# Mixtures, gathers and a router step of a mixture-of-experts kernel set to other places in the program

## The chip, the cores and the metric

The kernel runs on one core of a Trainium2 chip. The metric is the device time of one execution in microseconds; below, "time" is the median of the runs shown, and "span" is the time from the first to the last instruction in one profiled execution. The engines are TensorE (PE; its weight loads are PEld), VectorE (DVE), ScalarE (ACT), GpSimd (POOL) and SyncE (SP), which only issues DMAs here.

## The reference

Input x is 8 batches of 1024 tokens with 512 features, all in 32 bit. The block is `x = x + attention(layernorm(x))`, then `x = x + experts(layernorm(x))`.

- Attention has 16 heads of 32. Queries, keys and values are sines and cosines (a table of 2048 steps with linear interpolation) of angles that are linear in the feature and in the token's place; then causal softmax and the sum over values, and a last sine plus cosine.
- Experts: a router (512 x 8) and softmax choose 2 of 8 experts for each token. Each expert takes the first 160 tokens of each batch that chose it (its capacity), so 1280 rows in all, computes `relu(rows @ W1 + b1) @ W2 + b2` with a hidden size of 2048, and the result times the gate is added to the token's row.

## The kernel before

**Attention.** 32 rounds, one for each batch and each chunk of 128 features. The router of a batch runs as a generator (`router`, L779) whose steps are spread over the rounds of the next batch. For the last batch it runs inside the experts' first part, as `ending` (L1503).

**Experts.** The rows of an expert are done in two parts: 768 rows (even parts, 0, 2, ...) and 512 rows (odd parts), so 16 parts. Each product of matrices is done with seven block products instead of eight, so rows, weights and results are mixed by sums and differences:

- `gather` (L1072) fetches a part's rows in tiles of 128 by indirect DMA on POOL (`fetch`, L1078), six tiles for an even part and four for an odd one. It transposes each on TensorE (L1117), copies it to `xe` on DVE (L1118) and mixes the rows on DVE (L1124 to L1127). The pool of fetched tiles, `gp`, has two buffers.
- `mix_w1` (L1144) makes four differences of a tile of W1 on DVE (L1153; in the first six groups of the first part on POOL).
- `layer1` (L1158) does one of eight groups of hidden features: seven products of 2 matmuls (L1169, 384 or 256 columns) and what follows them on DVE and ACT (L1184 to L1202).
- `mix_w2` (L1043) mixes the eight tiles of W2 on DVE, four operations a tile (L1050 to L1053).
- `layer2` (L1205) does a block of 128 x 2 rows: seven products of 8 matmuls (L1214, 256 columns), sums, bias and gate on DVE (L1230, L1231, L1246 to L1258), and an indirect DMA with addition for each half (`send`, L1236). An even part has three blocks, an odd one two. The first three products of a block use W2 as loaded; the fourth uses the third output of `mix_w2`.

The profile counts a 32-bit matmul as two records.

**What sets the order.** On PE, DVE, ACT and SP the program's own order holds (`manual_schedule`). POOL's instructions are put in order by a scheduler, but for some that are marked to stay in program order: the gathers of parts 1 and 2, the sends of part 0, and the W1 mixtures on POOL. Work beside the products is generators: after each product, `product` calls `next` on them, so a `yield` is a distance of one product. In layer two the generator is the gather of the next part; in the first part's layer one it is `ending`, which ends by loading the slot table (`fetch_slots`, L989). Behind the first part's layer one, `find_rows` (L1069) turns the slot table into row numbers for the odd parts' gathers, on DVE.

PSUM: `ps_p` has six buffers, one for a product; `ps_tr` two, for transposes and the last router. In the last router, `rows` (L807) normalises a tile of tokens on DVE and stores it through SP (L813), `features` transposes two tiles on TensorE (L823) and copies them on ACT (L824), and `sums` multiplies by the router's weights (L869). The buffers for normalised tiles (`xn2`) are two.

The loop over parts, as it stands (L1309 to L1323):

```python
elif i == 0 and q == NHQ - 2:
    mixes = mix_w2(0)
    for _ in range(2):
        next(mixes)
...
if i == 0:
    find_rows(1)
rest(mixes)
aside = start(gather(i + 1), box) if i + 1 < len(chunks) else iter(())
if i == 0:
    aside = behind(2, aside)
for block in range(nh):
    layer2(i, block, hs, aside)
rest(aside)
if i + 1 < len(chunks):
    mix_w1(i + 1, 0)
```

Of the kernel before, what the change touches and what calls it, by code (L numbers as in the profile page):

```python
# [73 lines left out]
def preln_attn_moe_kernel(  # L74
# [133 lines left out]
    def two_banks():  # L208
        return ps_sc.tile([P, 2, 512], F32, name="ps_s")
# [515 lines left out]
    def some(count, *gens):  # L725

        for gen in gens:
            while count and next(gen, 0) is None:
                count -= 1
# [51 lines left out]
    def router(b):  # L781
# [11 lines left out]
        last = b == B - 1  # L793
# [22 lines left out]
        def features(g):  # L816

            xT = row2.tile([P, NCH, 2 * P], F32, name="xT", bufs=1)
            if last:
                for i, xn in enumerate(ahead):  # L820
                    ps = pools["ps_tr"].tile([P, NCH, P], F32, name="ps_t")
                    for c in range(NCH):
                        nc.tensor.transpose(ps[:, c, :], xn[:, c * P : (c + 1) * P], ident)  # L823
                    copy(xT[:, :, i * P : (i + 1) * P], ps)  # L824
            else:
                ps = two_banks()
                for i, xn in enumerate(ahead):
                    for c in range(NCH):
                        at = (NCH * i + c) * 64
                        by_halves(ps[:, :, at : at + 64], xn[:, c * P : (c + 1) * P])  # L830
                for a in range(2):
                    copy(  # L832
                        xT.rearrange("p c (i a q) -> p i c a q", a=2, q=64)[:, :, :, a, :],
                        ps[:, a, :].rearrange("p (i c q) -> p i c q", i=2, q=64),
                    )
            return xT
# [47 lines left out]
        lg = None  # L884
        for g in range(NTT // 2):
            xT = features(g)
            if g + 1 < NTT // 2:
                if not last:
                    yield
                next_rows(g)  # L890
            yield
            lg = sums(g, xT, lg)
            yield
# [124 lines left out]
    chunks = []  # L1018
# [55 lines left out]
    def gather(i):  # L1074

        e, j0, nh = chunks[i]
        def fetch(xg, j):
            ins = nc.gpsimd.indirect_dma_start(  # L1078
                out=xg, out_offset=None, in_=xn2_d[i % 2],
                in_offset=bass.IndirectOffsetOnAxis(ap=source[:, e, j0 + j, None], axis=0),  # L1080
            )
            if i in (1, 2):
                tc.keep_in_program_order(ins)
            return xg

        def fetch_next(j):
            return fetch(pools["gp"].tile([P, D], F32, name="xg"), j)

        there = []
        if i == 0:  # L1090

            t = row2.tile([P, NCH, 2 * P], F32, name="xT", bufs=1).rearrange("p c t -> p (c t)")
            places = [row2.tile([P, D], F32, name="xn2") for _ in range(2)]
            places += [t[:, :D], t[:, D:]]
            there = [fetch(xg, j) for j, xg in enumerate(places)]
            yield None
            there += [fetch_next(j) for j in (4, 5)]
        xe = pools["xep"].tile([P, NCH, 2, HALF], F32, name="xe")
        for j in range(2 * nh):
            if len(there) == j:  # L1100
                there.append(fetch_next(j))
            if j or i:
                yield None
            xg = there[j]
            dst = xe[:, :, j // nh, j % nh * P : (j % nh + 1) * P]
            if i == 0:
                ps = two_banks()[:, :, : NCH * 64]
                for c in range(NCH):
                    by_halves(ps[:, :, c * 64 : (c + 1) * 64], xg[:, c * P : (c + 1) * P])
                nc.vector.tensor_copy(  # L1110
                    dst.rearrange("p c (a q) -> p c a q", a=2),
                    ps.rearrange("p a (c q) -> p c a q", q=64),
                )
            else:
                ps = pools["ps_tr"].tile([P, NCH, P], F32, name="ps_t")
                for c in range(NCH):
                    nc.tensor.transpose(ps[:, c, :], xg[:, c * P : (c + 1) * P], ident)  # L1117
                nc.vector.tensor_copy(dst, ps)  # L1118
        n = nh * P
        a11, a12 = xe[:, :2, 0, :n], xe[:, 2:, 0, :n]  # L1120
        a21, a22 = xe[:, :2, 1, :n], xe[:, 2:, 1, :n]
        s = pools["xep"].tile([P, 3, 2, HALF], F32, name="xe_s")
        s2, s3, s4 = (s[:, k, :, :n] for k in range(3))
        TT(s3, a11, a21, ALU.subtract)  # L1124
        TT(a21, a21, a22, ALU.add)
        TT(s2, a21, a11, ALU.subtract)
        TT(s4, a12, s2, ALU.subtract)  # L1127
        yield a11, a12, s4, a22, a21, s2, s3
# [13 lines left out]
    def mix_w1(i, q):  # L1142
        w = w1_tiles.pop((i, q))
        t = pools["t1p"].tile([P, 4, 2, P], F32, name="t1")  # L1144
        b11, b12 = w[:, :2, 0, :], w[:, :2, 1, :]
        b21, b22 = w[:, 2:, 0, :], w[:, 2:, 1, :]
        t1, t2, t3, t4 = (t[:, k, :, :] for k in range(4))


        apart = i == 0 and q < 6  # L1150
        mix = nc.gpsimd.tensor_tensor if apart else TT
        for to, x1, x2 in ((t1, b12, b11), (t2, b22, t1), (t3, b22, b12), (t4, b21, t2)):
            done = mix(to, x1, x2, ALU.subtract)  # L1153
            if apart:
                tc.keep_in_program_order(done)
                mixed.append(done.ins)
        t1_tiles[i, q] = b11, b21, b22, t1, t2, t3, t4
# [114 lines left out]
    def experts_begin():  # L1272
# [6 lines left out]
        mix_w1(0, 0)  # L1279

    def experts(ending):
        pools["hp"] = to_end.pool("hp", NHQ, **right)
        pools["ps_tr"] = to_end.pool("ps_tr", 2, space=PSUM, reuse_waits="tile")
        pools["ps_p"] = to_end.pool("ps_p", 6, space=PSUM, reuse_waits="tile")
        box = first_parts
        mixes = loads = iter(())
        for i, (e, j0, nh) in enumerate(chunks):
            parts, box = box[0], [None]
            hs = []
            for q in range(NHQ):  # L1290
                if i or q != NHQ - AHEAD - 1:
                    load_ahead(i * NHQ + q + AHEAD)
                some(3, loads)
                if q + 1 < NHQ:
                    mix_w1(i, q + 1)
                if q > 1:
                    for _ in range(1 if i else 3):
                        next(mixes, None)
                hs.append(layer1(i, q, parts, [ending]))
                if i == 0 and q == NHQ // 2:  # L1300
                    rest(ending)
                    to_router.close()
                    for name, bufs in (("w2p", NHQ), ("yp", 3), ("bp", 1)):
                        pools[name] = to_end.pool(name, bufs, reuse_waits="tile", **left)
                    load_ahead(NHQ - 1)
                    load_b2(0)
                    rest(load_w2(0))
                elif i == 0 and q == NHQ - 2:
                    mixes = mix_w2(0)  # L1309
                    for _ in range(2):  # L1310
                        next(mixes)
            if i == 0:
                find_rows(1)
            rest(mixes)
            aside = start(gather(i + 1), box) if i + 1 < len(chunks) else iter(())
            if i == 0:

                aside = behind(2, aside)
            for block in range(nh):
                layer2(i, block, hs, aside)  # L1320
            rest(aside)
            if i + 1 < len(chunks):
                mix_w1(i + 1, 0)  # L1323
            if i % 2 and e + 1 < E:
                load_b2(e + 1)
                loads = load_w2(e + 1)
                mixes = mix_w2(e + 1)
# [20 lines left out]
    last = None  # L1348
# [4 lines left out]
    for n in range(NCK):  # L1353
# [144 lines left out]
        last = (es[1], halves1, pos_n)  # L1498
# [5 lines left out]
    def ending():  # L1504

        o_st = o_pre(NCK - 1, pos_n)
        scatter(NTT * TOPK // 2, together=True)
        yield
        sine(o_st[1])
        square(o_st[0])  # L1510
        for _ in range(3):
            yield
        for _ in o_post(NCK - 1, o_st):
            yield
        yield
        for name in router(B - 1):
            if name == "tiles":
                scatter(together=True)

            for _ in range({"tiles": 6, "places": 5}.get(name, 1)):  # L1520
                yield
        fetch_slots(B - 2)
        scatter(together=True)
        fetch_slots(B - 1)
# [33 lines left out]
```

## Time and profile before

| | |
|---|---|
| time, median of 3 runs | 3299.44 us (3293.29 to 3300.38) |
| the profiled execution's own time | 3283.79 us |
| its span | 3282.1 us |
| mean granted TensorE clock | 0.996 |
| attention, up to about | 1272 us |
| first part, layer one | 1273 to 1362 us |
| first part, layer two | 1367 to 1445 us |
| an even and an odd part together, later on | 246.7 us |
| DMA, share of 16 engines: the queue of SP, that of POOL | 28.6%, 7.5% |
| gather, from issue to landing: least, median, most | 3.2, 3.4, 4.8 us |
| send, the same | 4.6, 4.9, 9.6 us |

How to read it: a row of the waits names the instruction that waited, the one that released it, the total, the number of times and the longest. A row of the timeline has start, length, engine, line, operation, output and inputs, count, and in brackets the idle time ahead of it and what ended it. A row of the windows has the busy time of each engine in a stretch, the TensorE clock that was granted as a share of full speed, and what the DMA engines did.

### The profile page before, as it was taken

The numbers are of one execution on the slowest core, as the hardware profiler recorded it, in microseconds if no ns is written. First come the engines' busy times: TensorE is split into PE (matmuls) and PEld (weight loads), VectorE is DVE, ScalarE is ACT, GpSimd is POOL, SyncE is SP. The second block draws the span as 40 slices with busy tenths as digits, with TensorE's granted clock in tenths as the row PEclk, the third lists the DMA queues.
The fourth block names the chain that finished last, engine by engine and source line by source line (L and its number), as shares of the span: only waits on it lengthen the run. The fifth ranks groups of instructions, "written<-read, shape, count | busy, mean of one in ns | idle before, by whom it ended". The sixth has DMA issues, their size and how long they took to land.

```text
span 3282.1 us, 48761 instructions
## 1 busy us (share of the span) xinstructions
PE 3191.8 (97%) x18942; PEld 2166.0 (66%) x18942; DVE 2252.1 (69%) x4961; ACT 1322.4 (40%) x1617; POOL 421.3 (13%) x387
## 2 busy tenths in 40 slices
PE   5999999999999999999999999999999999999998
PEld 2444444444444444688688688688688688688687
DVE  7888888778787675755855755755755755845844
ACT  7888887878787874111111111201201201201201
POOL 2000202011110213311011011011011011011010
PEclk9999999999999999999999999999999999999999
DMA  5435454553545353423323323323322322322321
GB/s 162 143 97 161 125 150 139 142 155 104 181 116 156 92 172 71 109 51 81 94 48 77 97 49 75 99 48 72 103 45 73 105 43 73 105 44 71 107 39 26
DMA packets 235254, 319.74 MB, mean 97 GB/s; under 512 B 22456, under 2 KB 155280, under 8 KB 222992
## 3 DMA queue, kind: packets, MB, share of 16 engines
q1 hardware_dynamic: 211664, 273.38, 28.6%
q0 software_dynamic: 22912, 43.22, 7.5%
q8 instruction: 150, 2.46, 0.3%
q14 instruction: 80, 0.66, 0.1%
q10 hardware_dynamic: 448, 0.02, 0.0%
HBM read 187.62 MB, written 61.82 MB: 76 GB/s over the span
## 4 chain that ended last, share of the span: by engine, by line
PE 73%; DVE 6%; issue 3%; ACT 1%; DMA 1%; SPq 0%; POOL 0%; POOLq 0%; DVEq 0%; ACTq 0%
PE ps_p L1214 28%; PE ps_p L1169 25%; PE av L713 9%; PE ps_s L679 8%; ACT e L699 1%; PE ps_t L1117 1%; PE ps_s L215 1%; DVE qk_f L520 1%; PE ps_s L693 1%; DVE t L1153 1%; DMA xg<-xn_d,source 1%; DVE qk_r L450 0%; DMA xn_d<-xn 0%; DVE xT L832 0%; DMA qk<-qk_r 0%
## 5 line engine op out<-in xcount | busy, mean ns | idle before, releaser
L699 ACT ACTIVATE e<-ps_s 128x1024 f32<-128x1024 f32 (+1 forms) x640 | 568.5, 937 | 192.7 <-PE ps_s L679 112.2
L679 PE MATMUL ps_s<-qk 64*128 64x512 f32 (+3 forms) x3072 | 596.5, 505 | 32.8 <-DMA qk<-qk_r 12.4
L1214 PE MATMUL ps_p<-w,hid 128*128 128x256 f32 x2560 | 570.3, 380 | 4.7 <-DVE hid L1187 4.7
L1214 PEld LDWEIGHTS ps_p<-w,hid 128*128 128x128 f32 x2560 | 485.0, 191 | 71.6 <-DVE hid L1187 5.3
L713 PE MATMUL av<-e,v 128*64 128x512 f32 (+3 forms) x3072 | 524.1, 490 | 0.0
L1214 PE MATMUL ps_p<-w_t,hid 128*128 128x256 f32 x1920 | 428.9, 379 | 0.0
L679 PEld LDWEIGHTS ps_s<-qk 64*128 64x128 f32 x3072 | 262.4, 188 | 219.1 <-issue 106.9
L1214 PEld LDWEIGHTS ps_p<-w_t,hid 128*128 128x128 f32 x1920 | 362.0, 190 | 47.6
L713 PEld LDWEIGHTS av<-e,v 128*64 128x64 f32 x3072 | 200.4, 137 | 283.8 <-issue 268.0
L1169 PE MATMUL ps_p<-xe_s,t 128*128 128x256 f32 (+1 forms) x1024 | 299.1, 435 | 3.6 <-DVE t L1153 3.6
L1169 PE MATMUL ps_p<-xe,w 128*128 128x256 f32 (+1 forms) x1024 | 298.8, 434 | 1.2 <-DVE hid L1187 1.0
L1169 PE MATMUL ps_p<-xe,t 128*128 128x256 f32 (+1 forms) x1024 | 296.8, 433 | 0.0
L764 POOL DMA_INDIRECT slot_d<-token,slot x128 | 158.0, 1235 | 981.4 <-issue 629.0
L1245 ACT COPY p<-ps_p 128x256 f32<-128x256 f32 x40 | 14.7, 368 | 610.1 <-PE ps_p L1214 610.1
L1169 PEld LDWEIGHTS ps_p<-xe_s,t 128*128 128x128 f32 x1024 | 194.2, 190 | 87.7 <-DVE t L1153 8.1
L1169 PEld LDWEIGHTS ps_p<-xe,w 128*128 128x128 f32 x1024 | 192.7, 190 | 84.3 <-DVE hid L1187 8.2
L1169 PEld LDWEIGHTS ps_p<-xe,t 128*128 128x128 f32 x1024 | 194.4, 190 | 80.9 <-issue 0.4
L1078 POOL DMA_INDIRECT xg<-xn_d,source x76 | 74.3, 978 | 1060.2 <-PE ps_t L1117 1045.7
L1236 POOL DMA_INDIRECT out_dram<-y,slots x80 | 126.5, 1581 | 649.3 <-DVE y L1231 620.2
L1184 ACT ACTIVATE p<-ps_p,b_t 128x256 f32<-128x256 f32 (+1 forms) x128 | 65.4, 511 | 328.3 <-PE ps_p L1169 177.2
L1188 ACT ACTIVATE hid<-hid 128x256 f32<-128x256 f32 (+1 forms) x128 | 60.1, 470 | 327.8 <-DVE hid L1187 327.8
L1201 ACT ACTIVATE hid<-hid,b_more 128x256 f32<-128x256 f32 (+1 forms) x128 | 71.8, 561 | 274.4 <-DVE hid L1200 274.4
(224 smaller groups left out, 3815.6 us busy)
## 6 DMA issues: line engine op xcount, KB each, us to landing
w<-in_L_ffn_W_dram SPq DMA_DIRECT2D x256, 256.0 KB, 3.3
w<-in_L_ffn_W_dram SPq DMA_DIRECT2D x64, 512.0 KB, 7.3
qk<-qk_c SPq DMA_DIRECT2D x124, 256.0 KB, 4.0
qk<-qk_r SPq DMA_DIRECT2D x124, 256.0 KB, 4.3
qk_base<-base_d SPq DMA_DIRECT2D x28, 1024.0 KB, 8.9
xn_d<-xn SPq DMA_DIRECT2D x72, 256.0 KB, 2.4
x_mid<-in_L_attn_x_dram SPq DMA_DIRECT2D x16, 1024.0 KB, 8.8
out_dram<-x_mid SPq DMA_DIRECT2D x8, 2048.0 KB
```

Of the source, the lines that this page charges most:

```text
L215: nc.tensor.transpose(turned[:, a, :], src[r, :], ident[r, r])
L679: nc.tensor.matmul(ps[:, a, at : at + w], lhsT=pair[r, 1, kb * P : (kb + 1) * P], rhs=pair[r, 0, q0 : q0 + w], start=at == 0, stop=not own ...
L699: nc.scalar.activation(e, ps[:, :, :n], AF.Exp, scale=UNIT * UNIT / math.sqrt(2 * DH))
L713: nc.tensor.matmul(av[a * 64 : (a + 1) * 64, q0 - 512 * h :], lhsT=vt[:, kb, 2 * pr + a, :], rhs=es[i][:, a, at : at + w], start=kb == 0, ...
L764: queued = nc.gpsimd.indirect_dma_start(out=slot_d[b], out_offset=bass.IndirectOffsetOnAxis(ap=idx, axis=0), in_=src, in_offset=None,)
L1078: ins = nc.gpsimd.indirect_dma_start(out=xg, out_offset=None, in_=xn2_d[i % 2], in_offset=bass.IndirectOffsetOnAxis(ap=source[:, e, j0 + j ...
L1169: nc.tensor.matmul(ps, lhsT=weights[:, k, :], rhs=rows[:, k, :], start=k == 0, stop=k == 1)
L1184: nc.scalar.activation(p1, product(b11, a11), AF.Identity, bias=b1_t[:, e * NHC + q : e * NHC + q + 1])
L1188: nc.scalar.activation(h11, h11, AF.Relu)
L1201: nc.scalar.activation(h12, h12, AF.Relu, bias=more)
L1214: nc.tensor.matmul(ps, lhsT=hs[k][:, part, cols], rhs=ws[k][weight], start=k == 0, stop=k == NHQ - 1,)
L1236: ins = nc.gpsimd.indirect_dma_start(out=out, out_offset=bass.IndirectOffsetOnAxis(ap=meta[:, e, jj[r], 0:1], axis=0), in_=ys[r], in_offse ...
```

## The change

Four places, all of order; no arithmetic is added or taken away.

1. `features(0)` of the last router is done one step earlier: `ending` waits five steps instead of six behind "tiles", and a `yield` is put behind the first `features`, so that the rows that follow keep their step.
2. `gather` of every part but the first: two tiles are fetched at the first step, then two steps pass before the first tile is transposed. The further tiles are fetched, in the program, right behind the transposes that free their buffer. Before, a tile was fetched one step ahead of its transposes.
3. In the first part, the three mixtures of W2 between `mix_w1(0, 7)` and the last group of layer one go; they are done with the rest, behind `find_rows(1)`. `some(2, mixes)` does the same two mixtures as the loop before it.

4. `mix_w1(i + 1, 0)` is done ahead of the last block of layer two instead of behind it.

```diff
@@ router: the loop over pairs of tiles
             xT = features(g)
+            if last and g == 0:
+                yield
             if g + 1 < NTT // 2:
@@ gather
             there += [fetch_next(j) for j in (4, 5)]
+        else:
+            there = [fetch_next(j) for j in range(2)]
+            yield None
+            yield None
         xe = pools["xep"].tile([P, NCH, 2, HALF], F32, name="xe")
         for j in range(2 * nh):
-            if len(there) == j:
-                there.append(fetch_next(j))
-            if j or i:
+            if j:
                 yield None
             xg = there[j]
@@ gather: behind the transposes and the copy of tile j
                 nc.vector.tensor_copy(dst, ps)
+            if len(there) < 2 * nh:
+                there.append(fetch_next(len(there)))
@@ experts: the loop over groups of layer one
-                if q > 1:
-                    for _ in range(1 if i else 3):
-                        next(mixes, None)
+                if i and q > 1:
+                    next(mixes, None)
@@
                     mixes = mix_w2(0)
-                    for _ in range(2):
-                        next(mixes)
+                    some(2, mixes)
@@ experts: layer two
             for block in range(nh):
+                if block == nh - 1 and i + 1 < len(chunks):
+                    mix_w1(i + 1, 0)
                 layer2(i, block, hs, aside)
             rest(aside)
-            if i + 1 < len(chunks):
-                mix_w1(i + 1, 0)
@@ ending
-            for _ in range({"tiles": 6, "places": 5}.get(name, 1)):
+            for _ in range({"tiles": 5, "places": 5}.get(name, 1)):
                 yield
```

On POOL the scheduler gives another order from the second part on. For an odd part's layer two (with the gather of the next even part) it was: four gathers (tiles three to six), a send, two gathers of the next odd part, three sends. It is: three gathers (tiles three to five), a send, a gather (tile six), a gather of the next odd part, a send, a gather of the next odd part, two sends.

## The prediction

> **What bounds the kernel now.** First the busy shares of the page, then the waits of TensorE from the last attention block on, then the timeline at the end of the first part's layer one, then busy time and granted clock in windows of 3.41 us.
>
> ```profile
> PE 3191.8 (97%) x18942; PEld 2166.0 (66%) x18942; DVE 2252.1 (69%) x4961; ACT 1322.4 (40%) x1617; POOL 421.3 (13%) x387
> ```
>
> TensorE is busy 97% of the span, and in the experts nearly without a gap: from 1548 us to the end it idles only at the W1 waits below. Of this change nothing can be gained but TensorE's waits, and they are few:
>
> ```profile
> PE ps_p L1214 <- DVE hid L1187: 4.7, 1, 4.7
> PE ps_p L1169 <- DVE t L1153: 3.6, 8, 0.6
> PE ps_t L1117 <- DMA xg<-xn_d,source: 3.3, 2, 1.8
> PE ps_t L869 <- ACT xT L824: 2.7, 1, 2.7
> PE ps_p L1169 <- DVE hid L1187: 1.0, 1, 1.0
> ```
>
> The columns are who waits for whom, us in total, times, longest. Each edit aims at one row: W2 mixtures at the first, W1 mixture at the second, gathers at the third, router step at the last two. Together they are 15.3 us, 0.46% of the time.
>
> **W1 mixture (L1153).** Four subtractions of 0.42 us go in front of the last block; they issue no DMA, and nothing else is added. TensorE waits for them eight times, in front of each part with 256 columns a product, where the third product comes 4 x 0.43 = 1.7 us after the start; with 384 columns the third comes after 2.6 us, and no wait is shown. In the new place DVE is mostly idle (5.6 us idle before L1249 at 1537 us) and TensorE may run six ps_p buffers of 3.46 us ahead. Late next is the first part of L1187, for which six more products have room. **-3.6 us**; if a buffer ran out instead the gain would be 0. I take the whole.
>
> **Gathers (L1078, L1117).** The instruction order shows what "sooner" comes to: POOL's order is the scheduler's, and a fetch needs only that its buffer's last tile is transposed, so most fetches stood early already. What moves is the transposes: each comes one product later. The two waits are at 1396.17 (1.50 us) and 1522.86 (1.81 us), both a part's last tile, whose fetch stands on POOL behind the first send of y (L1236). In the second, product five ends at 1513.10, the send starts at 1516.34, the fetch at 1518.25, and the tile is used at 1522.86: 9.8 us after product five. Before, it is due 7.8 us after it (two products of 3.46, two transposes of 0.44); afterwards three of each stand between, 11.7 us. Margin 1.9 us there, 2.2 us at the first (9.45 us). **-3.3 us**. In the later even parts the new order also puts the sixth fetch behind that send, where before it stood ahead; by the same count the 1.9 us cover it. Bounds: -3.3 and, with the cover gone, the last rival. The other sends lose nothing: each waits for the landing of the send before anyway.
>
> **W2 mixtures (L1050 to L1053).** Here is the largest wait, and I expect little.
>
> ```profile
> 1366.13 0.55 DVE L1187 TENSOR_TENSOR hid<-p,ps_p 128x384 f32<-128x384 f32 x1
> 1366.67 1.58 POOL L989 DMA_DIRECT2D slots<-slot_d  x2 [5.67 <-DMA slot_d<-token,slot]
> 1366.73 12.81 PE L1214 MATMUL ps_p<-w,hid 128*128 128x256 f32 x48 [4.66 <-DVE hid L1187]
> 1372.61 0.17 DVE L1069 TENSOR_SCALAR source<-slots 128x32 int32<-128x32 int32 x1
> 1372.70 0.42 DVE L1050 TENSOR_TENSOR w_t<-w 128x256 f32<-128x256 f32 x1
> ...
> 1379.37 3.62 PE L1214 MATMUL ps_p<-w_t,hid 128*128 128x256 f32 x16
> ```
>
> Five mixtures of 1.715 us (L1050 starts at 1360.99, 1362.70, 1364.42) stand ahead of L1187; TensorE is through layer one at 1362.07 and waits for the buffer that L1187 frees. Then three products need no mixture, and the fourth (the 1379.37 row) needs the third output of all eight; it ends at 1382.83. Afterwards only two mixtures stand ahead: L1187 starts 3 x 1.715 = 5.14 us sooner, at 1360.99, and the wait goes. Layer two starts at 1362.07 and its fourth product is reached at 1362.07 + 3 x 3.46 = 1372.45. But six mixtures now stand behind find_rows (L1069), which stands in DVE's queue behind layer one, and it needs the slot loads L989. These start at 1366.67 and 1367.3, released by POOL's scatters and not by DVE, and land 3.8 and 3.3 us later in the table of DMA issues: about 1370.6. So DVE, free at 1367.6, waits 3 us where it waited for nothing. The eighth mixture's third output is then there at 1370.8 + 5 x 1.715 + 1.33 = 1380.7, and the fourth product ends at 1381.2, 1.6 us sooner, not 7.
>
> The clock takes that back. Before, the wait is followed by half clock:
>
> ```profile
> 1296.74:1300.15 3.41, 0.92 (x9) 0.28 (x9) 1.84 (x4) 2.06 (x5) 0.00 (x0) 0.90 1.00 89
> 1300.15:1303.56 3.41, 3.41 (x11) 2.09 (x12) 1.01 (x2) 0.92 (x3) 0.00 (x0) 0.60 1.01 201
> 1361.59:1365.00 3.41, 0.48 (x2) 0.00 (x0) 3.21 (x9) 0.00 (x0) 0.00 (x0) 0.90 0.29 14
> 1365.00:1368.41 3.41, 1.68 (x4) 1.40 (x5) 3.13 (x8) 0.52 (x1) 1.58 (x2) 0.50 0.51 145
> 1368.41:1371.83 3.42, 3.42 (x11) 2.68 (x11) 2.94 (x7) 0.96 (x2) 0.00 (x0) 0.60 0.09 2
> ```
>
> The columns are window, length, busy PE, PEld, DVE, ACT, POOL, granted clock, DMA, GB/s. A window in which TensorE is busy 0.92 or 0.48 of 3.41 us is followed by half clock; 1.68 did not end it, a full window did. It cost 2.4 us before (the 48 matmuls took 12.81 us where 10.4 is the rate of 3.46 a product). Afterwards TensorE gets one step of 0.43 us per 1.715 us from 1373.7 to 1380.7, busy about a quarter, as in the first row; I expect the cut again, the last step at half rate (1381.6), and 2.4 to 5.7 us of half clock behind it, 2.0 us lost in the middle: 1383.6 against 1382.8. **+0.7 us.** Bounds: -1.6 with the clock up, -4.7 if the slots were there at 1367.6, +2.2 with the longest cut.
>
> The Trainium skill ("TensorE: Matmul & The Clock Gate", Part 1) says the clock halves after a wholly idle window of about 3.4 us. The trace has it after a gap of 2.66 us with 27% of the window busy. By the page, the trickle of steps would hold the clock up; the second rival is that case.
>
> **Router step (L823, L824, L869).** Eight transposes and two copies on ACT (0.53 us each) move one product forward, ahead of L1201, which ends an idle 2.38 us on ACT; the row stores on SP keep their step. The waits of 2.7 and 1.0 us go, but TensorE meets the next ones early. Rows five and six (L807) wait 4.82 us on DVE for the stores of rows three and four, issued at 1299.29, landed 6.97 us later in the chain of waits, and TensorE's transposes of them at 1307.4 and 1308.47 (a wait of 0.47) follow. None of that moves, and from 1322 to 1366 us DVE is the chain. **0 us**; bounds -1 (part of the 3.7 survives) and +1 (half clock displaced behind 1308).
>
> **Sum.** -3.6 - 3.3 + 0.7 + 0 = -6.2 us. The profiled execution took 3283.79 us (span 3282.1 and 1.7 around it), 15.6 us under the median of 3299.44; waits counted in it are taken off that median: 3293.2 us, 0.19% faster. About 0.2% (6.6 us) is what a measurement of this kernel can tell from no change.
>
> **Rivals.**
> - As forecast, -4 to -8 us (3291.4 to 3295.4): chance 0.42.
> - The clock stays up in the trickle: -3.6 - 3.3 - 1.6 = -8.5, 3290.9. For it: no gap is over 1.3 us. Against: the first window row. 0.18.
> - The W2 edit gains 4.7 (DVE starts its six mixtures at 1367.6 and the fourth product ends at 1378.1) because the slots are there earlier: -3.6 - 3.3 - 4.7 = -11.6, 3287.8. For it: only the landing of two small loads stands against it. Against: their issue at 1366.67 hangs on POOL's sixteen scatters, which nothing here moves. 0.12.
> - The gather edit doesn't do what it says: the last tile still stands behind the send and is still late, and its 3.3 us stay: -2.9, 3296.5. 0.14.
> - Slower: the sixth fetch, now behind the send in seven more parts, lands late. The traced gather behind a send took 4.6 us from issue to use; margin 1.9. Sends take up to 9.6 us to land; a gather that took as long would be 5.0 - 1.9 = 3.1 us late, 7 times, 22 us: 3315. From 6.5 us it costs something, from 8.3 us it makes the kernel slower by 0.2%. Against: gathers land in 3.2 to 4.8 us. 0.14.
>
> **Chances and range.** Faster by over 0.2%: the second and third cases and under half of the first, 0.49. Slower: the last, 0.13 that it passes 0.2%. Within 0.2%: the rest, 0.38. The range runs from just under the third case to the fourth with a few us for the spread of the runs (3293.29 to 3300.38): 3286.5 to 3299.5; the last case is left out.
>
> **What would show it.** Right: no wait for L1153 (now L1159) or the gather; L1069's successor idle about 3 us for the slot loads; TensorE waiting for w_t in the first part's fourth product, half clock behind it; DVE still waiting 4.8 us for the row stores. Wrong: gather waits in the parts from 1740 us on, POOL's sixth fetch late behind the send; or a first part whose fourth product ends near 1378.

## The result, and the profile after

The changed kernel takes **3284.47 us** (median of 6 runs, 3283.06 to 3286.53), the kernel before beside it 3298.95 us (6 runs, 3293.29 to 3300.38): ratio 0.9961, 95% interval 0.9950 to 0.9971, so 9.6 to 16.5 us less. Forecast were 6.2 us less; the lower end of the range was 3286.5.

The profiled execution of the changed kernel took 3283.24 us (span 3281.5). That is only 0.6 us less than the profiled one of before (span 3282.1), and yet the experts, from the first product of layer one to the last product, take 1984.35 us instead of 1999.01. The 14 us between are attention's, which no edit touches: the experts start at 1287.55 us in this profile and at 1273.49 in that of before. So spans can't be compared here; lengths of stages can. They are differences of the start times of TensorE's matmuls in the trace.

The page's first line and the waits of TensorE from 1290 us on, of the kernel after (who waits for whom, us in total, times, longest):

```profile
PE 3189.7 (97%) x18942; PEld 2166.0 (66%) x18942; DVE 2254.8 (69%) x4961; ACT 1322.2 (40%) x1617; POOL 422.8 (13%) x387
```

```profile
PE ps_p L1175 <- issue: 2.5, 1, 2.5
PE ps_t L823 <- DVE xn L807: 2.4, 2, 1.3
PE ps_p L1220 <- DVE w_t L1054: 1.5, 2, 1.0
PE ps_t L852 <- DVE prior L943: 0.7, 1, 0.7
PE ps_t L823 <- DVE prob L876: 0.6, 2, 0.4
PE ps_t L869 <- ACT xT L824: 0.5, 1, 0.5
```

Of the five rows at which the edits aimed, four are gone and L869 shrank from 2.7 to 0.5. New are the wait for w_t, as forecast, 2.4 us for the router's rows (L807), and a stop at L1175 that nothing in the program explains ("issue": no releaser is named).

Lines of the kernel after, with those of before in brackets: L1071 (L1069) row numbers, L991 (L989) slot loads, L1159 (L1153) W1 mixture, L1175 (L1169) and L1220 (L1214) the products of layer one and two, L1190 (L1184) ScalarE's first step behind a group, L1193 (L1187) VectorE's, L1054 (L1052) the third step of a W2 mixture.

### The profile page after: what moved, and what is told of

Its sections match the earlier page's. It is cut to its first block, busy times and chain, and to the rows that moved or that the text cites. A ratio compares the mean times of both kernels' runs of the same rounds, so it can differ in the third digit from the quotient of the medians.

```text
span 3281.5 us, 48762 instructions
## 1 busy us (share of the span) xinstructions
PE 3189.7 (97%) x18942; PEld 2166.0 (66%) x18942; DVE 2254.8 (69%) x4961; ACT 1322.2 (40%) x1617; POOL 422.8 (13%) x387
## 4 chain that ended last, share of the span: by engine, by line
PE 77%; DVE 5%; ACT 1%; DMA 1%; issue 1%; another core or an unknown queue 0%; SPq 0%; POOLq 0%; DVEq 0%; ACTq 0%
PE ps_p L1220 29%; PE ps_p L1175 28%; PE av L713 9%; PE ps_s L679 8%; PE ps_t L1121 1%; ACT e L699 1%; PE ps_s L215 1%; DVE qk_f L520 1%; PE ps_s L693 1%; DVE qk_r L450 1%; DMA xn_d<-xn 0%; DVE v L450 0%; DVE xn L807 0%; DVE xT L832 0%; DMA qk<-qk_r 0%
## 5 line engine op out<-in xcount | busy, mean ns | idle before, releaser
L1220 PE MATMUL ps_p<-w,hid 128*128 128x256 f32 x2560 | 567.0, 379 | 0.0
L1220 PEld LDWEIGHTS ps_p<-w,hid 128*128 128x128 f32 x2560 | 484.1, 190 | 66.3
L1220 PE MATMUL ps_p<-w_t,hid 128*128 128x256 f32 x1920 | 430.5, 379 | 1.5 <-DVE w_t L1054 1.5
L1220 PEld LDWEIGHTS ps_p<-w_t,hid 128*128 128x128 f32 x1920 | 361.2, 190 | 49.5 <-DVE w_t L1054 2.3
L1175 PE MATMUL ps_p<-xe,w 128*128 128x256 f32 (+1 forms) x1024 | 297.8, 434 | 0.0
L1175 PE MATMUL ps_p<-xe_s,t 128*128 128x256 f32 (+1 forms) x1024 | 296.9, 433 | 0.0
L1175 PE MATMUL ps_p<-xe,t 128*128 128x256 f32 (+1 forms) x1024 | 296.8, 433 | 0.0
L1175 PEld LDWEIGHTS ps_p<-xe,t 128*128 128x128 f32 x1024 | 194.4, 190 | 80.9 <-issue 0.4
L1175 PEld LDWEIGHTS ps_p<-xe_s,t 128*128 128x128 f32 x1024 | 194.3, 190 | 80.7 <-issue 0.4
L1175 PEld LDWEIGHTS ps_p<-xe,w 128*128 128x128 f32 x1024 | 193.4, 190 | 80.9 <-DVE hid L1193 3.7
L1190 ACT ACTIVATE p<-ps_p,b_t 128x256 f32<-128x256 f32 (+1 forms) x128 | 65.4, 511 | 336.9 <-PE ps_p L1175 177.2
```

Source lines behind the costliest of these rows:

```text
L1175: nc.tensor.matmul(ps, lhsT=weights[:, k, :], rhs=rows[:, k, :], start=k == 0, stop=k == 1)
L1190: nc.scalar.activation(p1, product(b11, a11), AF.Identity, bias=b1_t[:, e * NHC + q : e * NHC + q + 1])
L1220: nc.tensor.matmul(ps, lhsT=hs[k][:, part, cols], rhs=ws[k][weight], start=k == 0, stop=k == NHQ - 1,)
```

## The experiments

The kernels ran on three chips: e1 to e4 on the first, e5 to e8 on the second, e9 to e16 on the third. On the third attention ends 10 to 15 us sooner than on the others, and before takes 3283 to 3285 us there instead of 3295.6, so times are compared only within one chip. The chips of the two first profiles are not known. Lengths in us; "part 0" is the first part, both layers. The ratios are of a kernel's time to that of before on the same chip, with a 95% interval.

| kernel | experts start | part 0 layer one | part 0 layer two | odd parts' layer one, sum of 8 | part 1 layer two | experts |
|---|---|---|---|---|---|---|
| before, first profile | 1273.49 | 93.24 | 78.25 | 394.33 | 52.98 | 1999.01 |
| after, first profile | 1287.55 | 89.72 | 76.28 | 387.19 | 50.98 | 1984.35 |
| e1 before | 1287.06 | 96.14 | 77.95 | 394.33 | 52.51 | 2001.09 |
| e2 W1 alone | 1285.81 | 95.93 | 78.55 | 387.20 | 52.63 | 1994.49 |
| e3 gathers alone | 1286.79 | 95.59 | 76.87 | 394.28 | 50.98 | 1997.89 |
| e4 W2 alone | 1287.82 | 91.26 | 77.24 | 394.33 | 52.53 | 1995.53 |
| e5 router alone | 1284.29 | 92.46 | 78.33 | 394.16 | 52.85 | 1997.88 |
| e6 before, loads spread | 1285.09 | 92.29 | 78.74 | 393.88 | 52.65 | 1997.89 |
| e7 W2, loads spread | 1286.11 | 90.62 | 83.39 | 393.89 | 52.57 | 2000.85 |
| e8 after, loads spread | 1284.64 | 89.85 | 81.49 | 386.83 | 50.98 | 1989.52 |
| e9 after without W2 | 1274.61 | 92.81 | 75.94 | 387.13 | 50.98 | 1986.89 |
| e10 three ahead | 1274.59 | 89.94 | 76.73 | 387.15 | 50.98 | 1984.86 |
| e11 spread, rows last | 1273.98 | 88.98 | 80.22 | 386.82 | 50.98 | 1987.31 |
| e12 joined | 1273.19 | 89.48 | 75.45 | 387.15 | 50.98 | 1983.13 |
| e13 before | 1273.56 | 92.31 | 77.57 | 394.29 | 52.66 | 1997.00 |
| e14 W2 alone | 1274.55 | 87.54 | 81.71 | 394.33 | 52.70 | 1996.46 |
| e15 after | 1274.28 | 87.31 | 80.00 | 387.21 | 50.98 | 1985.70 |
| e16 joined | 1272.43 | 88.84 | 75.46 | 387.22 | 50.98 | 1982.65 |

All later stages but part 1's layer two and the odd parts' layer one are alike in every kernel to 0.4 us.

**One edit at a time.** e1 is the kernel before; e2, e3, e4 and e5 have one of the four edits each:

```diff
 e2:  if block == nh - 1 and i + 1 < len(chunks):
+         mix_w1(i + 1, 0)
 e3:  there = [fetch_next(j) for j in range(2)]
+     yield None
+     yield None
 e4: -    for _ in range(1 if i else 3):
+     if i and q > 1:
          next(mixes, None)
 e5:  xT = features(g)
+     if last and g == 0:
+         yield
```

> The kernel before, unchanged, a second profile. Theory A (the 15 us between its profile, 3283.8, and its runs, 3299, lie in attention, which happened to be short in that one execution; the change saves 14.7 us of experts): experts start near 1287 us and take 2008.6 us again, span near 3296. Theory B (the runs of before lose their 15 us in the experts, and the change takes nothing but that): experts start at 1273 us and take about 2023 us.

Measured: 3295.05 us, ratio 0.9995 (0.9986 to 1.0005); attention ends where it does in the kernel after, as theory A has it.

> Only the W1 mixture of the next part in front of the last block. Theory A: the waits row shows half of each wait, the stage lengths show 0.83 to 1.02 us in each of eight odd parts' layer one; all of it goes with this edit alone, odd parts' layer one 48.35 us, sum -7.1 us. Theory B: this edit is worth the 3.6 us of the waits row, and the rest of the odd parts' gain belongs to the new order of gathers.

Measured: 3288.53, ratio 0.9973 (0.9961 to 0.9984). The odd parts' layer ones are 7.1 us shorter in all, twice what the row of the waits shows (theory A).

> Only the gathers a step sooner. Theory A: -1.7 us in the first part's layer two and -2.0 us in the second's, nothing later, odd parts' layer one stays 49.2 us: -3.7 us. Theory B: odd parts' layer one falls by 0.4 us too, -7 us in all. If the sixth gather comes late behind the send in later parts: odd parts' layer two over 50.98 us.

Measured: 3292.82, ratio 0.9987 (0.9978 to 0.9996); the experts are 3.2 us shorter, 1.5 of it in part 1's layer two and 1.6 in part 0. The odd parts' layer one keeps its length, so theory B falls.

> Only the W2 mixtures behind layer one. The prediction's theory: the wait of 4.7 us goes, the fourth product waits for the slot table through find_rows and the mixtures, half clock behind it: first part +0.7 us (-1.6 with the clock up). Rival, from the profile of the change, where an instruction load of 2.6 us stalled TensorE for 2.5 us in the last group: without such a stall the first part is 4 to 5 us shorter, with it 2.4 us.

Measured: 3293.84, ratio 0.9989 (0.9980 to 0.9998); part 0 is 5.6 us shorter. The "instruction load" of that expectation did not stall TensorE: in the trace's DMA records of the kernel after it runs from 1376.19 to 1378.83 us, and TensorE goes on at 1375.87.

> Only the router step. The prediction's theory: the two waits go (2.7 and 1.0 us) and come back at the next transposes, which hang on the row stores: first part 0 us. Rival: the three groups behind it start 1.4 us sooner and keep it: first part's layer one -1.4 us.

Measured: 3294.41, ratio 0.9999 (0.9990 to 1.0008). The time can't tell 1 us, and no profile of plain before was taken on this chip. Against e6 (before with other loads, below) layer one is 0.2 us longer and its fourth group starts at the same place (39.4 us, in e6 39.3), so the rival's gain of 1.4 us is not there.

**ScalarE's stop.** In e1 to e4 and in the profile after, ScalarE stands still once in the last group of part 0's layer one, for 3.1 to 5.6 us, and the profile names no instruction of the program as releaser ("remote"). The timeline of e1, before (start, length, engine, what, and in brackets the idle ahead of it and its releaser):

```profile
1376.63 0.58 ACT L1184 ACTIVATE p<-ps_p,b_t 128x384 f32<-128x384 f32 x1 [3.10 <-remote]
1377.26 2.93 PE L1169 MATMUL ps_p<-xe_s,w 128*128 128x384 f32 x4 [2.77 <-ACT p L1184]
1383.20 12.31 PE L1214 MATMUL ps_p<-w,hid 128*128 128x256 f32 x48 [3.01 <-DVE hid L1187]
```

and of the kernel after:

```profile
1375.24 0.58 ACT L1190 ACTIVATE p<-ps_p,b_t 128x384 f32<-128x384 f32 x1 [5.57 <-remote]
1375.87 1.56 PE L1175 MATMUL ps_p<-xe_s,w 128*128 128x384 f32 x4 [2.48 <-issue]
1382.51 0.17 DVE L1071 TENSOR_SCALAR source<-slots 128x32 int32<-128x32 int32 x1
```

In e1 the stop (2.77) and the wait for the five mixtures (3.01) add up on TensorE; in the profile after only the stop is left, and L1071 finds its slots landed.

What came late is TensorE's signal. A product that is done updates a semaphore, a counter on which the engine that needs the product waits, and the trace has the time of each update. In the kernel after, the first six of the group's seven products end 1.29 us apart, from 1366.95 to 1373.40 us; their updates are recorded at 1375.16, 0.08 us before ScalarE starts, and then five within 0.24 us, 1375.92 to 1376.16. In e15 each of the group's updates is recorded 0.01 us behind the end of its product. So by its rows TensorE had done the products in time, and the engines that waited for them were told late.

My first theory laid the stop on the loads of W2, all issued at once two groups before. e6 to e8 spread them:

```diff
-    rest(load_w2(0))
+    loads = load_w2(0)
```

> The kernel before with the eight loads of W2 of the first part spread over groups five to seven of layer one (three, three, two) instead of one burst behind group four. In the second profile of before, ACT stands still for 3.1 us in the last group of the first part, released by nothing that the profile names, and TensorE waits 2.8 us for it. Theory A (the burst of loads delays ACT's instructions): the stop goes, layer one of the first part 93.2 us as in the first profile instead of 96.1. Theory B (the stop has nothing to do with the loads): 96 us again.

Measured: 3293.96, ratio 0.9996 (0.9987 to 1.0005). Layer one is short, but not because the stop has gone. ScalarE's step L1184 (in e5 L1186) in e5, whose loads are not spread, in e6, and in e13, before on the third chip:

```profile
1369.48 0.58 ACT L1186 ACTIVATE p<-ps_p,b_t 128x384 f32<-128x384 f32 x1 [2.41 <-issue]
```

```profile
1370.24 0.58 ACT L1184 ACTIVATE p<-ps_p,b_t 128x384 f32<-128x384 f32 x1 [2.53 <-PE ps_p L1169]
```

```profile
1356.10 0.56 ACT L1184 ACTIVATE p<-ps_p,b_t 128x384 f32<-128x384 f32 x1
```

On the second chip ScalarE stands still too, for 1.8 to 2.5 us in e5 to e8, and behind it six updates of TensorE are recorded within 0.3 us. TensorE does not wait for it there. **This theory fell**: the stop is as long with the loads spread as without.

> The W2 edit alone, with the same spread loads. If the stop of ACT goes, this is the edit under the conditions that the prediction took: its theory says the first part is +0.7 us (-1.6 with the clock up) against the spread kernel without the edit, with TensorE waiting for w_t in the fourth product and DVE waiting 3 us for the slot table. Rival (slot table lands sooner, no half clock behind the trickle): -4 to -5.5 us.

Measured: 3296.61, ratio 1.0003 (0.9994 to 1.0012). Against e6 part 0 is 3.0 us longer: layer one 1.7 shorter, layer two 4.7 longer. VectorE waits 2.20 us for the slots, and the fourth product takes 8.97 us instead of 3.89. That is dearer than the +0.7 expected and the bound of +2.2; 1.4 us of it is there before the edit can act, where the fourth group starts (40.7 against 39.3 us).

> All four edits with the same spread loads. Theory A: TensorE's 2.5 us stop in the last group goes, part of it comes back as a longer wait for w_t in the fourth product: first part 164.5 us against 166.0. Theory B: the first part as without the spread, 166.0 us.

Measured: 3286.84, ratio 0.9973 (0.9963 to 0.9983); the fourth product 8.12, the fifth 6.11. TensorE does not stop, as in all four kernels on this chip, but part 0 takes 171.34 us, where theory A had 164.5: layer two is 5.2 us longer than in the profile after.

**What the W2 edit is worth in the whole change, and what its wait hangs on.** e9 is the change without edit 3. The others:

```diff
 e10: three mixtures ahead
-    some(2, mixes)
+    some(3, mixes)
 e11: loads spread as in e6, and the row numbers behind the mixtures
-    if i == 0:
-        find_rows(1)
     rest(mixes)
+    if i == 0:
+        find_rows(1)
 e12: three ahead, row numbers behind, and
-    rest(load_w2(0))
+    loads = load_w2(0)
+    some(2, loads)
```

> The change without its W2 edit: W1 mixture, gathers and router step are moved, the five W2 mixtures stay in front of the last group's sums. Theory 1 (in ordinary runs ScalarE stops in the last group of the first part's layer one, the wait for the five mixtures comes on top, and the W2 edit takes that wait away): the first part's layer one is 94.5 to 96.5 us instead of 89.7 in the changed kernel, its layer two as there or up to 0.6 shorter, the time 3287.5 to 3290. Theory 2 (the prediction: the W2 edit costs 0.7 us): layer one 93 to 94, layer two 75.5, the time 3283.8, no difference from the changed kernel. Both: odd parts' layer one 48.35, part one's layer two 50.98.

Measured: 3272.92, ratio 0.9965 (0.9951 to 0.9978). Nothing stops on this chip, so theory 1's case did not come, and TensorE waits 4.7 us for hid as in the first profile of before; the stages are near theory 2's (92.81 and 75.94). Beside the whole change on the same chip (e15, below) part 0 is 168.75 us against 167.31: in the whole change the edit is worth 1.2 us of the experts there (1986.89 against 1985.70).

> The changed kernel with three W2 mixtures ahead of the last group's sums instead of two. Theory 1: in the changed kernel's profile VectorE stood idle 2.32 us there because of ScalarE's stop, so the third mixture (1.715 us) costs nothing in layer one (89.7, within the 0.7 by which the groups before it vary), and the fourth product's wait for w_t, 1.5 us in two pieces, goes: layer two 74.6 to 75.0 instead of 76.28, time 1 to 2 us below the changed kernel's 3284.5. Theory 2 (no stop matters; each mixture ahead delays the last sums, 4.66 us for five): layer one 1.2 to 1.7 longer, layer two 1.3 shorter, time equal.

Measured: 3270.69, ratio 0.9958 (0.9944 to 0.9971). Without the stop the third mixture costs 1.2 us in front of layer two; VectorE waits 1.44 us for the slots, and the fourth product takes 5.81 us. That is theory 2's price in layer one, but not its gain in layer two: 76.73, where theory 1 had 74.6 to 75.0.

> The changed kernel with the W2 loads spread over three groups, and the row numbers (find_rows) computed behind the six mixtures instead of ahead of them, to be compared with the same kernel with the row numbers ahead (layer one 89.85, layer two 81.49). Theory 1 (the prediction's mechanism: the mixtures stand behind the wait for the slot loads, and TensorE's trickle and the half clock follow from it): VectorE's wait of 1.76 us goes, the mixtures start that much sooner, the fourth product ends 1.8 us sooner, and with less half clock behind it the layer two is 78.0 to 79.8. Theory 2 (the six mixtures alone pace the fourth product, the wait of VectorE is covered or replaced): layer two 81 to 82. Both: layer one within 0.7 of 89.85, nothing later changes, since the second part's first row fetch starts two products into layer two.

Measured: 3271.63, ratio 0.9955 (0.9942 to 0.9969). With the row numbers behind the mixtures the fourth product takes 3.45 us, but the first and second now wait 3.7 us in all for the last two loads of W2. So the fourth product's length supports theory 1, and the layer two (80.22, expected 78.0 to 79.8) tells nothing.

> A version that joins what the runs point to: the changed kernel with three mixtures ahead, the row numbers behind the mixtures, and the W2 loads spread but two of them at once (so that all have been issued two groups before the end of layer one). Theory 1: no stop of ScalarE, so the third mixture now costs up to 1.2 us (4.66 us was the wait for five): layer one 89 to 91; the last mixture's third output comes 1.76 + 1.72 = 3.5 us sooner than with spread loads alone, the fourth product waits 0 to 1.5 us, no half clock behind it: layer two 75.5 to 77.5. Sum 164.5 to 168.5 against the changed kernel's 166.0, time 3283 to 3286. Theory 2 (the loads do not matter, ScalarE stops for another reason): the stop of 3 to 5.6 us is there again, layer one 91 to 94, sum 167 to 170, time 3286 to 3289.

Measured: 3268.88, ratio 0.9952 (0.9938 to 0.9965); part 0 is 164.93 us. The third chip has no stop, so this does not test theory 2.

**The change and its W2 edit where nothing stops.** e13 is before, e14 is e4, e15 the whole change, e16 is e12, on one chip.

> The kernel before, profiled once more. If the stop goes with the chip (theory 1): either all four kernels of this call show experts starting at 1273 to 1275 us and no idle of ScalarE released by remote in the last group of the first part's layer one, and this one has layer one 92.5 to 94, layer two 78.3, time about 3285; or all four start at 1284 to 1288 and this one has a stop of 3 to 5 us, layer one 95.5 to 96.5, time about 3296. If it goes with the kernel or with chance (theory 2), the four are mixed.

Measured: 3283.40, ratio 1.0000 (0.9991 to 1.0009). None of the four stops, nor did e9 to e12: ScalarE's step follows the one before it without idle time in all eight. All start the experts at 1272.4 to 1274.6.

> W2 edit alone. Without ScalarE's stop, by the prediction's mechanism (VectorE waits for the slot table, six mixtures pace the fourth product): layer one 88.0 to 89.3, VectorE's wait for the slots 2.5 to 3 us, the fourth product 8.3 to 9.2 us instead of 3.89, half clock behind it or not, layer two 81.5 to 83.5; part 0 is 169.5 to 172.5 against 171.5 of before, -2 to +1 us. By the rival (the edit takes away a wait of 4.7 us and nothing comes back): 88.6 + 73.5 to 75, -8 us. With the stop: as in the first run of it, layer one 91.3, layer two 77.2.

Measured: 3281.73, ratio 0.9994 (0.9985 to 1.0003): part 0 169.25 us against 169.88 in e13. VectorE's wait is 1.50 us, where 2.5 to 3 were expected. The timeline of e14 shows the chain that the prediction told:

```profile
1369.24 0.18 DVE L1069 TENSOR_SCALAR source<-slots 128x32 int32<-128x32 int32 x1 [1.50 <-DMA slots<-slot_d]
...
1375.88 0.70 PE L1214 MATMUL ps_p<-w_t,hid 128*128 128x256 f32 x2 [1.01 <-DVE w_t L1052]
...
1377.59 0.70 PE L1214 MATMUL ps_p<-w_t,hid 128*128 128x256 f32 x2 [1.01 <-DVE w_t L1052]
...
1379.31 0.91 PE L1214 MATMUL ps_p<-w_t,hid 128*128 128x256 f32 x2 [1.01 <-DVE w_t L1052]
```

VectorE waits for the slot loads; TensorE then takes one step for every 1.715 us of mixture. The windows of e14 there, within 0.3 us of where the granted clock changes (window, length, busy PE, PEld, DVE, ACT, POOL, granted clock, DMA share, GB/s):

```profile
1376.00:1379.40 3.40, 1.37 (x5) 0.57 (x5) 3.19 (x9) 0.00 (x0) 0.00 (x0) 1.00 0.00 0
1379.40:1382.80 3.40, 3.40 (x11) 2.82 (x12) 2.44 (x6) 0.00 (x0) 0.94 (x1) 0.54 0.00 0
1382.80:1386.20 3.40, 3.40 (x18) 2.95 (x18) 0.15 (x1) 0.00 (x0) 0.00 (x0) 0.96 0.28 77
```

TensorE is busy 40% of a window, its gaps no longer than 1.01 us as the profile counts them, and the clock of the next is 0.54; it is exactly half from 1379.67 to 1383.08. The fifth product takes 4.99 us instead of 3.89.

> The whole change, profiled and timed again. Without the stop, by the prediction's mechanism: layer one 88.0 to 89.3, fourth product 8.3 to 9.2, layer two 79.5 to 81.5, part 0 167.5 to 170.8, about what the change without its W2 edit had without the stop (168.75), so 3272 to 3274 where before has 3285 and that had 3272.9. By the rival: 88.6 + 73 to 74.5. With the stop: part 0 166, time 3283 to 3286.

Measured: 3271.04, ratio 0.9960 (0.9946 to 0.9974); L1071 waits 1.60 us, the fourth product takes 7.93, the fifth 5.14; part 0, 167.31 us, and the time come out a little under what was expected. The largest waits of TensorE in e15:

```profile
PE ps_p L1220 <- DVE w_t L1054: 3.0, 3, 1.0
PE ps_t L823 <- DVE xn L807: 2.8, 3, 1.2
```

> The joined version (three mixtures ahead, row numbers behind the mixtures, two W2 loads at once and the others spread) once more: part 0 164.5 to 165.5 with or without a stop on this chip (its first run had 164.93), and a time 1.5 to 4 us below the whole change of this call. Rival: on a chip with stops it stops too, 167 to 170, no difference in time.

Measured: 3266.69, ratio 0.9953 (0.9939 to 0.9966). The waits of TensorE for W2 and what stands behind it, in e16:

```profile
PE ps_p L1220 <- DVE hid L1193: 1.2, 1, 1.2
...
PE ps_p L1220 <- DVE w_t L1054: 0.5, 1, 0.5
```

1.7 us of waits are left where e15 has 3.0 and half clock behind them; the experts take 1982.65 us, 3.05 less than in e15. The medians stand 4.4 us apart, a little over the 1.5 to 4 expected, but the two intervals overlap, and the version has not run on a chip where ScalarE stops.

## Why the prediction was wrong, step by step

| step | forecast | third chip (no stop) | first chip (stop) |
|---|---|---|---|
| W1 mixture | -3.6 | -7.1 (e13, e15) | -7.1 (e1, e2) |
| gathers | -3.3 | -3.2 (e13, e15) | -3.2 (e1, e3) |
| W2 mixtures | +0.7 | -0.6 (e13, e14) | -5.6 (e1, e4) |
| router step | 0 | -0.4 to +0.4 (what is left) | not separated |
| experts in all | -6.2 | -11.3 (e13, e15) | -16.7 (e1, profile after) |

On the third chip the gathers are part 1's layer two, 52.66 to 50.98, and part 0's product with the late tile, 5.39 to 3.89. Part 0 falls by 2.57 in all; less 1.50 and 0.63 leaves 0.44 for the router; with the 1.44 that part 0 differs by between e9 and e15 in place of 0.63 it is 0.37 the other way. Both are less than the start of part 0's fourth group varies without any edit (39.2 in e13 to 40.3 us in the first profile). The last row on the right joins e1 with the first profile after, whose chip is not known to be the same; the three terms above it add up to 15.9. The timed gains are 14.5 us (9.6 to 16.5) for the result and 12.5 (8.5 to 17.7) on the third chip.

**W1 mixture: right cause, the term mis-sized by half. This is the step that failed on every chip.** The prediction took 3.6 us from the row of the waits: eight waits, seven of 0.43 and one of 0.6. The timeline at the start of part 3's layer one, before:

```profile
1694.08 1.89 PE L1169 MATMUL ps_p<-xe,w 128*128 128x256 f32 x8
1696.40 1.99 PE L1169 MATMUL ps_p<-xe_s,t 128*128 128x256 f32 x8 [0.43 <-DVE t L1153]
1698.23 1.89 PE L1169 MATMUL ps_p<-xe,t 128*128 128x256 f32 x8
```

and at the same place in the kernel after:

```profile
1699.65 1.89 PE L1175 MATMUL ps_p<-xe,w 128*128 128x256 f32 x8
1701.38 1.89 PE L1175 MATMUL ps_p<-xe_s,t 128*128 128x256 f32 x8
```

Two products that wait for nothing start 1.73 us before the next; the row's length of 1.89 is a modelled end that lies 0.16 behind the next start. Idle time is counted from that end, so 2.32 - 1.73 = 0.59 us late shows as 0.43, and the next pair, 1.83 instead of 1.73, shows none. That makes 0.69 us; another 0.14 goes at the start of the last group, where two matmuls start 0.25 and 0.32 us after the one before instead of 0.216. The whole layer one is 0.83 us shorter in most parts (49.18 to 48.35). All of this could be read before the result: 56 products at half of 1.73 us are 48.4, and the stage took 49.18. With 7.1 in place of 3.6 the forecast gain is 9.7 us (3289.7): just inside the measured 9.6 to 16.5, but 5.2 us above the median of the result. The W2 term failed too: +0.7 was forecast, and it measured -0.6 where TensorE does not stop and -5.6 where it does. Which of the two the timed runs had is not shown, but the profile after has the stop.

**Gathers: right**, in size and in its working. No gather is waited for after the change, and in the parts from 1740 us on no stage grows: the slower rival, a sixth fetch late behind the send, did not come. Nor did the rival that the edit does nothing (e3).

**W2 mixtures: the mechanism right where nothing stops; the forecast's sign missed by 1.3 us there.** In e14 against e13 layer one ends 4.77 us sooner (forecast 4.66), VectorE waits 1.5 us for the slots (forecast 3), the fourth product ends 2.0 us sooner (forecast 1.6), half clock behind it takes 1.1 us back (forecast 2.4) and a gather that is late by more another 0.3. Net -0.6, within the bounds of -4.7 to +2.2; with the loads spread, on the second chip, it was +3.0 (e7), of which 1.4 stands ahead of the edit. The rival that the clock stays up is refuted there: the fifth product of e14 takes 4.99 us. In the profile after and in e4, where the fourth product waits 1.5 and 0.2 us, the clock does stay up and the fifth takes 3.89. The prediction's windows did not stand where the clock changed: in before it is half from 1299.50 to 1302.91 and from 1364.35 to 1371.18 us, behind windows in which TensorE is busy 0.75 and 1.13 of 3.41 us. By the Trainium skill ("TensorE: Matmul & The Clock Gate", Part 1) the clock halves after an idle window of about 3.4 us; the window of e14 above, 40% busy and without a gap over 1.01 us, was followed by the cut all the same.

On the first chip the edit is worth 5.6 us, by what the first profile of before does not show. Part 0 of before is 4.2 us longer with the stop (174.09 in e1, 169.88 in e13; 0.9 of it are there before the stop, where the fourth group starts), since the wait for five mixtures follows it. The edited kernel loses nothing (168.50 in e4, 169.25 in e14): TensorE reaches layer two 3.7 us later than in e14, VectorE finds the slots landed, does its mixtures while TensorE is still late, and the fourth product takes 4.33 us instead of 8.41. So the edit does not take the stop away, it hides it. The prediction's third rival had -4.7 by slots that land sooner. Here their loads start no sooner (91.3 us behind the experts' start, in e14 89.1); VectorE comes to them later.

**Router step: right**, within the bounds of 1 us. Its waits of 2.7 and 1.0 gave way to 2.4 us for the rows (L807), as told; VectorE still waits 4.6 us for the row stores (forecast 4.8).

**The basis.** The prediction took -6.2 us off the median and not off the profiled execution, which was right; but it did not ask why the two were 15.6 us apart. The first profile of before is like those of the third chip (experts from 1273.5, no stop); the timed runs are, by their times, like those of the other two chips, which no profile of them shows. With W1 at 7.1 and W2 at -0.6 to -5.6, the same sum gives 3288.4 to 3283.4, and the result, 3284.47, lies between. None of the rivals had both misses, and none went below 3287.8.

**Open**: what holds TensorE's updates back. In e1 to e8 and in the profile after, 39 to 51 of TensorE's some 2220 updates are recorded over 0.25 us late or not at all; in the other nine profiles it is one at most. So it came in all eight profiles of two chips and in none of the eight of the third. That it goes with the chip is likely but rests on three chips, and its cause was not found.

## What to carry to other kernels

Take the price of a repeated wait from the length of its stage, less the number of products times the start-to-start rate, and not from a row of waits whose idle time begins at a modelled end. Where a profile and the median of the runs stand further apart than the effect looked for, find the stage that differs before using either. Work that is moved off one wait can come back at the next: here six mixtures behind a look-up that waits 1.5 us for a DMA, with the half clock and a gather that follow, gave back 4.1 of the 4.8 us that were won. Where a row names no releaser ("remote", "issue"), compare the time of the signal with the end of the work that sends it, before laying the stop on the engine that waits.

## What the runs showed of the hardware

- TensorE's clock was halved behind a window that was 40% busy with no gap over 1.01 us, in e14 and in e15. In the profile after, two such waits of 0.45 and 1.01 us were followed by a fifth product of 3.89 us, without a cut. The changes of the clock lie whole windows of 3.41 us apart. Counted in these windows over the matmul and clock records of all 18 traces, from 40 us on and from full clock: each of the 71 windows in which TensorE was busy under 40% was followed by half clock, 10 of the 15 from 40 to 51%, and none of the 16,867 above.
- The same program had attention 10 to 15 us shorter on one chip than on two others. In all nine profiles whose experts start after 1284 us, VectorE waits 7.6 to 7.8 us for TensorE's sums in the last rounds of attention (L748), and 1.96 us at that place in the others. The releaser is "remote" in five of them and TensorE in e1 to e3 and e6, as in these rows of the waits of the kernel after and of e1. This one wait is 5.8 us of attention's difference, and a late update of TensorE ends it (1268.94 us in the kernel after, L748 starts at 1268.96); the rest was not followed up.

```profile
DVE rec L748 <- remote: 7.8, 1, 7.8
```

```profile
DVE rec L748 <- PE ps_s L679: 7.8, 1, 7.8
```
